# A hand-written order of all compute engines in the blocks of a gated state-space mixer

## The chip, the cores and the metric

The kernel runs on one core of one Trainium2 chip. The metric is the device time of one execution in microseconds, as a median over runs of the same kernel. TensorE (PE in the profile, its weight loads PEld) multiplies matrices into PSUM, VectorE (DVE) and ScalarE (ACT) work element by element, GpSimd (POOL) does too, and SyncE (SP) issues most DMAs. Each engine works through its own list of instructions in order and waits on semaphores for the others.

## What is computed

The reference is a transformer block on `x` of 4 x 256 rows of 512: attention, a sparse feed-forward, a state-space mixer and the feed-forward again, each added to `x`. The change lies in the mixer alone:

```
proj = norm(x) @ in_proj_w.T                 # gate (8192), x, B, C (8192 + 2*8*128), dt (128 heads)
xBC  = silu(conv1d(xBC, 4 taps) + conv_b)    # along time, per channel
hs, Bm, Cm = split(xBC)                      # 128 heads of 64, 8 groups of B and C, 128 wide
y    = ssd(hs, A, Bm, Cm, D, dt)             # y_i = sum_{j<=i} (C_i.B_j) exp(cum_i - cum_j) dt_j x_j + D x_i
g    = y * silu(gate)
g    = g * rsqrt(mean over each group of 1024 of g*g + eps) * norm_w
out  = g @ out_w.T                           # 8192 -> 512
```

In exact terms the reference goes through chunks of 32 steps. The kernel takes the quadratic form of the last but third line over all 256 steps of a sequence: positions `j` after `i` must add nothing (the mask).

## The kernel before, in words

The mixer's 8192 inner channels are 64 blocks of 128 (two heads each); 8 blocks are a group, which shares one B and one C. Products of two fp32 matrices are done as three fp32r matmuls of split operands (`split`: a rounded upper part by ScalarE, L105, and the rest by a subtraction on VectorE, L106; `mm3`, L113 to L115). So every weight, from `win` (tile `wr`) or `wout` (`wor`) and every recalled piece of `g` (`gr`) is split first, into `w`, `wo` and `gh`.

Block `i` goes through these steps:

- `projected`: x and then the gate of the block, 24 matmuls of 128x512 each, from the normed input `mx` into a PSUM tile `pp`.
- `conv`: ScalarE scales (L981), VectorE adds three taps (L988), ScalarE takes silu (L996) into `x2`. For B and C the same (`bc`, L993).
- `rows`, `differences`: for each head a row of cumulated sums is read from DRAM (`r`, L1031). VectorE subtracts columns (L1043, L1047), GpSimd adds the mask of -3e38 (`past`, L1044) on the four diagonal pieces, ScalarE takes exps (L1052 direct, L1056, L1057) into `em`. `weighted` (L1061) multiplies by the group's scores `gm`, which `scores` makes from B and C (L1013, copied by L1021).
- `turned`: 8 transposes of `x2` on TensorE (L1072), scaled by dt on VectorE (L1073) into `xd`.
- `product` (L1089): 64 small matmuls of `em` and `xd` into `pyy`; `gated` adds D x (L1101), multiplies by the gate's silu `gt` (L1211, L1104), spills `gb` to DRAM (L1106, issued by SP) and sums squares (ScalarE L1111 and L1113, GpSimd L1114).
- Out products of the group before: `recall` reads a spilled half (L1150), `partial` multiplies 24 matmuls into `pog`, `scaled` (L1162) adds them to `x`. There are 8 of them per group, one for each 128 rows. `root` (L1135 to L1141) makes the group's factor.

The loop `for i in range(NB + 1)` (L1198) writes block `i`'s x and gate with block `i-1`'s product. Of a group's eight blocks the first (`i % 8 == 0`) has no out product of the group before, the second has two (`PER`), the others one. B of the next group is projected behind block 6 of a group and C behind block 7, with their scores. This text doesn't fix the order: a planner places each engine's instructions by costs and due times, and only some are pinned. TensorE, VectorE, ScalarE, GpSimd and SP all get their lists this way in the mixer.

[...] two `pp` tiles of two banks each, one `pyy` of two banks, and a pool `ps` (tag "m") of two single banks that transposes, scores, sums and out products all share. `acc`, `gt` and `xd` have one buffer, `x2` two, `em` three, `r` four.

Of the kernel before, what the change touches and what calls it, by code (L numbers as in the profile page):

```python
# [9 lines left out]
F32 = mybir.dt.float32  # L10
F32R = mybir.dt.float32r
# [24 lines left out]


COLS = {}
_at = 0
for _name, _w in (  # L40
    ("ident", 128), ("neg", 128), ("rot", 128), ("bdk", 2), ("bdv", 128), ("idx", 1), ("past", 64),
):
    COLS[_name] = (_at, _at + _w)
    _at += _w
# [5 lines left out]
def constants():  # L50
# [8 lines left out]
    put("past", np.where(np.arange(Q)[None, :] < r[:, None] % Q, -3e38, 0.0).astype(np.float32))  # L59
# [18 lines left out]
def hybrid_kernel(  # L78
# [705 lines left out]
    def mixer(feed, later):  # L784
        with ExitStack() as es, ExitStack() as inner:
# [25 lines left out]
            def prepare(i):  # L811

                for n in range(i, i + 3):
                    fetch(n)
                if i < NW and i not in pieces:
                    pieces[i] = [pw.tile([P, KC, P], F32R, name=f"w{j}", tag=f"w{j}") for j in range(2)]
                    split(pieces[i], raws.pop(i), nc.gpsimd if i < 5 else nc.vector)
# [9 lines left out]
            past = w1.tile([P, Q], F32, name="past")  # L827
            load(past, cst[:, COLS["past"][0] : COLS["past"][1]])
# [9 lines left out]
            nc.gpsimd.memset(w1.tile([P, 360], F32, name="fill1"), 0.0)  # L838
# [64 lines left out]
            reset = p2.tile([P, NT], F32, name="reset", tag="sq")[:, :512]  # L903
# [69 lines left out]
            silus = []  # L973

            def conv(pp, ch, inner):
# [3 lines left out]
                    else po_.tile([P, NT], F32, name="bc", tag="gb", bufs=3)  # L979
# [12 lines left out]
                if not inner:  # L992
                    silus.append(nc.scalar.activation(acc, acc, AF.Silu).ins)  # L993
                    return acc
                x2 = p2.tile([P, NT], F32, name="x2", tag="x2", bufs=2)
                silus.append(nc.scalar.activation(  # L996
                    pair(x2).rearrange("p k u i -> p u k i"),
                    acc.rearrange("p (u k i) -> p u k i", u=2, i=Q), AF.Silu,
                ).ins)
                return x2  # L1000

            def scores(bt, ct):

                gm = p2.tile([P, 20, Q], F32, name="gm", tag="gm")
                for j in range(2):
                    for cs in ((0, 1), (2, 3)):
                        pg = ps.tile([P, 512], F32, name="pg", tag="m")
                        at = 0
                        for c in cs:
                            n = (4 - c) * Q  # L1010
                            for u in range(2):
# [4 lines left out]
                                )  # L1016
                            at += n
                        at = 0
                        for c in cs:
                            n = (4 - c) * Q  # L1020
                            nc.vector.tensor_copy(  # L1021
                                piece(gm, j, c), pg[:, at : at + n].rearrange("p (k i) -> p k i", i=Q)
                            )
                            at += n
                return gm

            def rows(h):

                r = p2.tile([P, 2 * L], F32, name="r", tag="r", bufs=4)
# [7 lines left out]
            def differences(h, r):  # L1037

                e = p2.tile([P, 20, Q], F32, name="em", tag="em", bufs=3)
                own, next_ = pieces_of(e, 0, 4, 4, 7), pieces_of(e, 1, 8, 2, 9)  # L1040
                rv = r.rearrange("p (j c i) -> p j c i", j=2, c=4)
                cv = col_t[:, h, :].rearrange("p (j c) -> p j c", j=2).unsqueeze(3)
                nc.vector.tensor_tensor(own, rv, cv.to_broadcast([P, 2, 4, Q]), ALU.subtract)  # L1043
                nc.gpsimd.tensor_tensor(  # L1044
                    own, own, past.unsqueeze(1).unsqueeze(1).to_broadcast([P, 2, 4, Q]), ALU.add
                )
                nc.vector.tensor_tensor(  # L1047
                    next_, rv[:, :, 1::2, :], cv[:, :, 0::2].to_broadcast([P, 2, 2, Q]), ALU.subtract
                )
                for j in range(2):  # L1050
                    for c in range(2):
# [3 lines left out]
                        )  # L1055
                nc.scalar.activation(next_, next_, AF.Exp)  # L1056
                nc.scalar.activation(own, own, AF.Exp)  # L1057
                return e
# [4 lines left out]
            def turned(n, x2):  # L1063

                xd = p2.tile([P, TT, P], F32, name="xd", tag="xd", bufs=1)
                for half in range(2):
                    yield xd
                    hs = slice(half * 4, half * 4 + 4)
                    tr = ps.tile([P, 4, P], F32, name="trx", tag="m")
                    for q in range(4):  # L1070
                        c = half * 4 + q
                        nc.tensor.transpose(tr[:, q, :], x2[:, c * P : (c + 1) * P], ident)  # L1072
# [6 lines left out]
                yield  # L1079
# [16 lines left out]
            def gated(n, x2, gt, py, sq):  # L1096

                gb = po_.tile([P, NT], F32, name="gb", tag="gb", bufs=3)
# [5 lines left out]
                nc.vector.tensor_tensor(gb, gb, gt, ALU.mult)  # L1104
                if n < NB - 1:
                    load(spill[(n // GB) % 2][n % GB], gb)  # L1106
                else:
                    last.append(gb)
                if sq is None:
                    sq = p2.tile([P, NT], F32, name="sq", tag="sq")  # L1110
                    nc.scalar.activation(sq, gb, AF.Square)  # L1111
                else:
                    nc.scalar.activation(x2, gb, AF.Square)  # L1113
                    (nc.gpsimd if n < NB - 1 else nc.vector).tensor_tensor(sq, sq, x2, ALU.add)  # L1114
                return sq
# [4 lines left out]
            def out_weights(g, k):  # L1120

                r = po_.tile([P, C], F32, name="wor", tag="wor", bufs=2)
                tc.keep_in_program_order(load(r, wout[g * GB + k]))
                n = g * GB + k
                w = [po_.tile([P, C], F32R, name=f"wo{j}", tag=f"wo{j}", bufs=GB) for j in range(2)]
                nc.scalar.activation(w[0], r, AF.Copy, scale=nw_s[:, n : n + 1])  # L1126
                nc.vector.scalar_tensor_tensor(
                    w[1], r, nw_s[:, n : n + 1], w[0].bitcast(F32), ALU.mult, ALU.subtract
                )
                return w  # L1130

            def root(sq):
                pq = ps.tile([P, TT], F32, name="pqs", tag="m")
                for t in range(TT):
                    nc.tensor.matmul(  # L1135
                        pq[:, t : t + 1], sq[:, t * P : (t + 1) * P], ones[:, 0:1], start=True, stop=True
                    )
                rg = rg_s.pop(0)
                rg_s.append(rg)
                nc.scalar.activation(rg, pq, AF.Sqrt, bias=eps, scale=1.0 / (GB * P))  # L1140
                nc.vector.reciprocal(rg, rg)  # L1141
# [233 lines left out]
```

## Time and profile before

| what | value |
| --- | --- |
| runs shown | 1930.27, 1933.32, 1936.76 us; median 1933.32 |
| the profiled execution | 1932.12 us, of which the span on the chip is 1930.3 |
| from 0 to 385 us (attention, feed-forward) | PE 343.1, DVE 251.8, ACT 238.1, POOL 112.5 busy, clock 0.96 |
| 385 to 1838 us (the mixer's blocks) | PE 1392.1, DVE 1172.6, ACT 1112.7, POOL 369.5 busy, clock 0.99 |
| 1838 to 1930 us (last out products, feed-forward) | PE 81.2, DVE 68.9, ACT 45.3, POOL 0 busy, clock 0.97 |
| GpSimd's mask, L1044, 128 of them | 229.9 us, mean 1800 ns (1272 to 3883) |
| table loads of ScalarE in the blocks | 265, each 1283 ns |
| VectorE's L1047, 128 of them | 409 ns at least, 419 median, 2611 at most |
| the three taps, L988 | 1241 to 1283 ns each |

The page's rows of groups give an engine, an operation, its operands by name, the count, the busy time with the mean of one, and behind a second bar how long the engine sat idle before it and what ended that. Rows in order of time give start, duration, engine, line, operation and operands; a bracket is the wait just before, with its releaser. A table load is the row in which ScalarE fetches the functions of another set: exp and silu lie in different sets here.

### The profile page before, as it was taken

Reading aid. Unit: us, or ns where it says so; the run is one execution under the profiler, and the core shown is the slowest. Engines: PE = TensorE matmul, PEld = TensorE weight load, DVE = VectorE, ACT = ScalarE, POOL = GpSimd, SP = SyncE. Lnnn points to the kernel's source line nnn. Section 1 sums busy time; section 2 is a strip of 40 time slices with the busy share of each in tenths; the row PEclk is TensorE's granted clock in tenths of the full one; section 3 lists DMA queues with packets and bytes.
Section 4 is the critical chain, followed back from the end, with each engine's and each line's share of the span. In section 5 each row is a group of like instructions: output and inputs, shape, how many; then the busy total and the mean of one; then the engine's idle time right before and its main releaser. Section 6 shows DMA issues by size and latency. Waiting matters only on the chain.

```text
span 1930.3 us, 33621 instructions
## 1 busy us (share of the span) xinstructions
PE 1816.3 (94%) x12882; PEld 1455.3 (75%) x12882; DVE 1493.3 (77%) x2157; ACT 1396.1 (72%) x2527; POOL 482.0 (25%) x380
## 2 busy tenths in 40 slices
PE   7999988889999999999999989999999999999997
PEld 6777767767677777787778778777887788778877
DVE  5666667688798879778878787877878878878877
ACT  6576675468898777787677777776787787677763
POOL 6332320013322222232222222222231232222200
PEclk9999999899999999999999999999999999999999
DMA  4000000033444434333434344443444434343241
GB/s 140 1 1 1 27 10 22 24 110 121 147 143 132 136 129 145 124 123 132 142 121 142 120 126 131 145 129 120 127 142 126 132 126 141 125 129 126 95 122 53
DMA packets 154834, 206.89 MB, mean 107 GB/s; under 512 B 14640, under 2 KB 79664, under 8 KB 154672
## 3 DMA queue, kind: packets, MB, share of 16 engines
q1 hardware_dynamic: 154672, 204.73, 33.7%
q8 instruction: 101, 1.65, 0.4%
q14 instruction: 61, 0.50, 0.1%
HBM read 169.03 MB, written 35.65 MB: 106 GB/s over the span
## 4 chain that ended last, share of the span: by engine, by line
PE 46%; DVE 21%; ACT 20%; issue 5%; DMA 4%; POOL 3%; SPq 0%; ACTq 0%; DVEq 0%; POOLq 0%
DVE acc L988 8%; PE pp L113 5%; PE pp L114 5%; PE pp L115 5%; PE pog L113 5%; PE pog L115 5%; PE pog L114 4%; ACT L996 2%; ACT x L996 2%; PE trx L1072 2%; PE pyy L1089 2%; ACT e L475 2%; DMA r<-cumd 2%; DVE em L1061 2%; POOL em L1044 2%
## 5 line engine op out<-in xcount | busy, mean ns | idle before, releaser
L1044 POOL TENSOR_TENSOR em<-em,past 128x512 f32<-128x512 f32 x128 | 229.9, 1800 | 1045.7 <-DVE em L1043 992.3
L113 PE MATMUL pp<-mx,w 128*128 128x512 f32 (+1 forms) x1160 | 467.0, 403 | 18.9 <-DVE acc L988 12.8
L115 PE MATMUL pp<-mx,w 128*128 128x512 f32 (+1 forms) x1160 | 454.3, 392 | 0.1
L114 PE MATMUL pp<-mx,w 128*128 128x512 f32 (+1 forms) x1160 | 453.9, 391 | 0.0
L1061 DVE TENSOR_TENSOR em<-em,gm 128x1280 f32<-128x1280 f32 x128 | 195.8, 1530 | 169.3 <-ACT em L1057 139.6
L113 PEld LDWEIGHTS pp<-mx,w 128*128 128x128 f32 x1160 | 218.8, 189 | 73.8 <-issue 13.4
L988 DVE SCALAR_TENSOR_TENSOR acc<-pp,cw_s,acc 128x1012 f32<-128x1012 f32 (+2 forms) x192 | 244.3, 1272 | 23.3 <-ACT acc L981 20.4
L115 PEld LDWEIGHTS pp<-mx,w 128*128 128x128 f32 x1160 | 218.9, 189 | 46.7 <-DVE w L106 0.5
L114 PEld LDWEIGHTS pp<-mx,w 128*128 128x128 f32 x1160 | 219.0, 189 | 40.6 <-issue 0.6
L113 PE MATMUL pog<-wo,gh 128*128 128x512 f32 x512 | 205.3, 401 | 2.5 <-ACT wo L1126 1.1
L1052 ACT ACTIVATE em<-r,end_t 128x128 f32<-128x128 f32 x512 | 169.2, 392 | 45.9 <-PE pyy L1089 45.2
L115 PE MATMUL pog<-wo,gh 128*128 128x512 f32 x512 | 200.1, 391 | 0.0
L114 PE MATMUL pog<-wo,gh 128*128 128x512 f32 x512 | 199.8, 390 | 0.0
L1089 PE MATMUL pyy<-em,xd 64*64 64x192 f32 (+3 forms) x4096 | 176.6, 310 | 13.9 <-DVE em L1061 13.9
L1089 PEld LDWEIGHTS pyy<-em,xd 64*64 64x64 f32 x4096 | 142.9, 138 | 58.5 <-issue 24.1
L996 ACT ACT_TABLE_LOAD x57 | 73.1, 1283 | 119.8 <-DVE acc L988 119.7
L105 ACT CAST w<-wr 128x512 fp32r<-128x512 f32 x144 | 88.3, 614 | 85.0 <-PE pp L114 81.1
L1114 POOL TENSOR_TENSOR sq<-sq,x 128x1024 f32<-128x1024 f32 x55 | 137.6, 2501 | 25.2 <-ACT x L1113 25.2
L475 ACT ACTIVATE e<-sc,nmx 128x256 f32<-128x256 f32 (+1 forms) x256 | 104.2, 442 | 21.0 <-DVE nmx L469 20.9
L113 PEld LDWEIGHTS pog<-wo,gh 128*128 128x128 f32 x512 | 96.1, 188 | 24.7 <-ACT rg L1140 2.0
L115 PEld LDWEIGHTS pog<-wo,gh 128*128 128x128 f32 x512 | 96.1, 188 | 20.8 <-DVE gh L106 0.3
L106 DVE TENSOR_TENSOR gh<-gr,gh 128x512 fp32r<-128x512 f32 (+1 forms) x128 | 86.0, 678 | 33.2 <-ACT gh L105 33.2
(294 smaller groups left out, 3463.3 us busy)
## 6 DMA issues: line engine op xcount, KB each, us to landing
wr<-in_win_dram SPq DMA_DIRECT2D x287, 256.0 KB, 2.9
r<-cumd SPq DMA_DIRECT2D x256, 128.0 KB, 3.0
spill<-gb SPq DMA_DIRECT2D x63, 512.0 KB, 2.6
gr<-spill SPq DMA_DIRECT2D x120, 256.0 KB, 3.2
wor<-in_wout_dram SPq DMA_DIRECT2D x64, 256.0 KB, 2.8
out_dram<-x SPq DMA_DIRECT2D x8, 256.0 KB, 2.4
x<-in_x_dram SPq DMA_DIRECT2D x1, 1536.0 KB, 8.9
gr<-spill SPq DMA_DIRECT2D x8, 192.0 KB, 2.8
```

What stands on the lines that cost most here:

```text
L105: nc.scalar.copy(hl[0], v)
L113: nc.tensor.matmul(o, lh, rh, start=(first and k == 0), stop=False)
L114: nc.tensor.matmul(o, lh, rl, start=False, stop=False)
L115: nc.tensor.matmul(o, ll, rh, start=False, stop=(last and k == n - 1))
L475: nc.scalar.activation(es_[c][:, 2 * j + pr, :], sc[:, j, :], AF.Exp, bias=nm[:, j : j + 1], accum_out=rs[:, c, h : h + 1],)
L988: nc.vector.scalar_tensor_tensor(av[:, :, d:], pv[:, :, : L - d], cw_s[:, ch, tap : tap + 1], av[:, :, d:], ALU.mult, ALU.add,)
L996: silus.append(nc.scalar.activation(pair(x2).rearrange("p k u i -> p u k i"), acc.rearrange("p (u k i) -> p u k i", u=2, i=Q), AF.Silu,).ins)
L1044: nc.gpsimd.tensor_tensor(own, own, past.unsqueeze(1).unsqueeze(1).to_broadcast([P, 2, 4, Q]), ALU.add)
L1052: nc.scalar.activation(piece(e, j, c, 2 - c, 2), rv[:, j, 2:, :], AF.Exp, bias=end_t[:, h, 2 * j + c : 2 * j + c + 1],)
L1061: nc.vector.tensor_tensor(e, e, gm, ALU.mult)
L1089: nc.tensor.matmul(py[d, u, j * L + c * Q : (j + 1) * L].rearrange("p (k i) -> p k i", i=Q), xd[us, 4 * j + c, d], piece(es2[hh], j, c)[us ...
L1114: (nc.gpsimd if n < NB - 1 else nc.vector).tensor_tensor(sq, sq, x2, ALU.add)
```

## The change

The planner no longer orders the blocks: a new function `block(i)` writes the instructions of one block for TensorE, ScalarE, VectorE and GpSimd in the order in which each engine is to take them (`manual_schedule`); SP's DMAs are still planned. Operations are cut so that they can be placed apart: `differences` and `exponentials`, the upper and lower part of each split, fetching and splitting, `silu` and `side_by_side`, `sums` and `root`, half projections.

- One out product stands in every block from block 9 on, with row tile `i % 8 - 1` (the last one of a group in the first block of the group after next). In the second block of a group it comes last.
- B of the next group is projected behind block 3 of a group and C behind block 4, both counted from 0; their convs stand in blocks 4 and 5, the scores in block 6.
- A block's exps are taken together at the start of the block after it, and its two silus together.
- The mask is no longer added: ScalarE clips the differences with relu (of the negative, then exp of the negative), and the scores `gm` are multiplied by a 0/1 triangle `tri` where they were copied.
- ScalarE issues the spill, two blocks later; `r` has two buffers for four; `gb` and `wor` have four; all weights of the start are split by GpSimd.

```diff
             def conv(pp, ch, inner):
...
-                if not inner:
-                    silus.append(nc.scalar.activation(acc, acc, AF.Silu).ins)
-                    return acc
+                return acc
...
-                            nc.vector.tensor_copy(
-                                piece(gm, j, c), pg[:, at : at + n].rearrange("p (k i) -> p k i", i=Q)
+                            nc.vector.tensor_tensor(
+                                piece(gm, j, c), apart(pg[:, at : at + n]), apart(tri[:, :n]), ALU.mult
                             )
...
-                nc.gpsimd.tensor_tensor(
-                    own, own, past.unsqueeze(1).unsqueeze(1).to_broadcast([P, 2, 4, Q]), ALU.add
-                )
...
+            def exponentials(h, e):
...
                 nc.scalar.activation(next_, next_, AF.Exp)
-                nc.scalar.activation(own, own, AF.Exp)
-                return e
+                nc.scalar.activation(own, own, AF.Relu, scale=-1.0)
+                nc.scalar.activation(own, own, AF.Exp, scale=-1.0)
+                if h + 2 < H:
+                    rr[h + 2] = rows(h + 2)
...
             def turned(n, x2):
...
+                trs = [ps.tile([P, 4, P], F32, name="trx", tag="m") for _ in range(2)]
+                for c in range(TT):
+                    nc.tensor.transpose(trs[c // 4][:, c % 4, :], x2[:, c * P : (c + 1) * P], ident)
...
+            def spilled(n, gb):
+                if n < NB - 1:
+                    nc.scalar.dma_start(spill[(n // GB) % 2][n % GB], gb)
...
+            def block(i):
+                g, gi = divmod(i, GB)
+                n = at["x", i]
...
+                out = (g - 1, gi - 1) if gi else (g - 2, TT - 1)
...
+                first_out = gi == 1
+                if i >= 2:
+                    spilled(i - 2, gbs[i - 2])
...
+                if late_:
+                    nc.vector.reciprocal(rgs[g - 1], rgs[g - 1])
+                    scaled(*late_.pop())
...
+                x_steps = projected("x", i)
+                next(x_steps)
+                next(x_steps)
+                if i:
+                    decays(i - 1)
+                waiting = [k for k in "bc" if k + "pp" in group]
+                for k in waiting:
+                    group[k] = conv(group.pop(k + "pp"), (NB if k == "b" else NB + G) + g + 1, False)
+                if i:
+                    turn(i - 1)
+                    weigh(i - 1)
+                acc = conv(next(x_steps), i, True)
+                if i >= 2:
+                    squared(i - 2, xs2.pop(i - 2), gbs.pop(i - 2))
+                done = outer(*out) if out and not first_out else None
+                lower.append(upper_piece(n + 2))
+                if g and gi >= 1:
+                    ss = {1: (1,), 2: (4, 5)}.get(gi, (2 * gi, 2 * gi + 1))
+                    lower.extend(upper_half(g - 1, s) for s in ss)
+                if g and gi == 1:
+                    lower.extend(upper_out((g - 1) * GB + k) for k in range(4, 8))
+                xs2[i] = side_by_side(acc)
+                for k in waiting:
+                    silu(group[k])
+                if done:
+                    scaled(*done)
+                lowered()
+
+                g_steps = projected("g", i)
+                next(g_steps)
+                if not done:
+                    next(g_steps)
+                if i:
+                    inner_products(i - 1)
+                if done:
+                    next(g_steps)
+                scoring = None
+                if gi == 6 and g + 1 < G:
+                    scoring = scores(group.pop("b"), group.pop("c"))
+                    gms[g + 1] = next(scoring)
+                    next(scoring)
+                    next(scoring)
+                pp = next(g_steps)
+                lower.append(upper_piece(n + 3))
+                if g and gi == 0:
+                    lower.append(upper_half(g - 1, 0))
+                    lower.extend(upper_out((g - 1) * GB + k) for k in range(4))
...
+                ems[i] = [differences(h) for h in (2 * i, 2 * i + 1)]
+                lowered()
...
+                nc.scalar.activation(gts[i], pp, AF.Silu)
+                if g and first_out:
+                    rgs[g - 1] = root(sums(g - 1))
+                    late_.append(outer(*out))
+                if gi in NEXT and g + 1 < G:
+                    group[NEXT[gi] + "pp"] = whole(projected(NEXT[gi], g + 1))
+                    upper_piece(n + 4)()
+
+            with tc.manual_schedule(
+                engines={e.engine for e in (nc.tensor, nc.scalar, nc.vector, nc.gpsimd)}
+            ):
+                for i in range(NB):
+                    block(i)
```

`decays(i)`, `turn(i)`, `weigh(i)` and `inner_products(i)` are block `i`'s exps, `turned`, `weighted` and `product` with `gated`. `projected` is now a generator that stops before, between and behind its two halves. `upper_piece`, `upper_half` and `upper_out` issue ScalarE's part of a split of `w`, `gh` and `wo` and return a function that issues VectorE's part and the fetch of a later one; `lowered()` calls those collected. `outer` is one out product, `NEXT` is `{3: "b", 4: "c"}`. Behind the loop stand the last block's exps, product and squares, the last out product of group 6 and the split of group 7's `wo`.

## The prediction

> **What bounds the kernel now.** I read the page's busy shares and slices first, then busy time by stretches, then TensorE's rows in order of time, and last the rows of ScalarE.
>
> ```profile
> PE 1816.3 (94%) x12882; PEld 1455.3 (75%) x12882; DVE 1493.3 (77%) x2157; ACT 1396.1 (72%) x2527; POOL 482.0 (25%) x380
> PE   7999988889999999999999989999999999999997
> PEclk9999999899999999999999999999999999999999
> ```
>
> TensorE (PE) leads, at nearly full clock. Its busy time counts overlapping matmuls, so what a full TensorE looks like must come from starts:
>
> ```profile
> 1016.69 0.39 PE L114 MATMUL pp<-mx,w 128*128 128x512 f32 x1
> 1016.92 0.39 PE L115 MATMUL pp<-mx,w 128*128 128x512 f32 x1
> 1017.23 2.41 PE L1089 MATMUL pyy<-em,xd 64*64 64x256 f32 x64
> 1019.58 0.50 PE L113 MATMUL pp<-mx,w 128*128 128x512 f32 x1
> ...
> 472.69:492.69 20.00, 18.42 (x134) 13.86 (x132) 14.82 (x20) 17.19 (x25) 7.03 (x5) 1.00 0.44 139
> 1371.33:1391.46 20.13, 20.05 (x145) 16.13 (x145) 16.33 (x20) 15.79 (x25) 5.80 (x3) 1.00 0.40 130
> ```
>
> A 128x512 matmul starts every 0.2275 us (20 of them in 4.55 us), though each row says 0.39. The 64 small ones of `product` cost 2.5 us with both changes of shape. The windows give busy PE, PEld, DVE, ACT, POOL: a block with an out product (1371 to 1391) is full of TensorE, while in group 0, without one (473 to 493), ScalarE is fullest and TensorE waits. The waits, in group 0 and then in one later group:
>
> ```profile
> 485.67 0.47 PE L113 MATMUL pp<-mx,w 128*128 128x512 f32 x1 [0.57 <-DVE acc L988]
> 488.01 1.09 PE L1072 MATMUL trx<-con,x 128*128 128x128 f32 x8 [0.28 <-ACT x L996]
> 494.06 0.50 PE L113 MATMUL pp<-mx,w 128*128 128x512 f32 x1 [0.73 <-ACT gt L1211]
> ...
> 1279.10 0.47 PE L113 MATMUL pp<-mx,w 128*128 128x512 f32 x1 [1.03 <-DVE acc L988]
> 1302.03 1.53 PE L1013 MATMUL pg<-bc 128*64 128x256 f32 x16 [2.67 <-ACT bc L993]
> 1322.92 4.07 PE L1089 MATMUL pyy<-em,xd 64*64 64x256 f32 x62 [2.52 <-DVE em L1061]
> ```
>
> Adding up TensorE's gaps over 0.25 us between 385 and 1930 gives 75 us: 26 before 590 (start and group 0), 46 in the later groups, 3 behind. All matmuls stay, so the change can win 75 us at most, and a few us of shorter gaps and of `product`s and scores cut in two, each with two more changes of shape. From block 9's `product` (606.05) to block 57's (1723.35) six groups take 1117.3 us, **186.2 each**.
>
> **TensorE's own work per group.** A block: 72 big matmuls x 0.2275 = 16.4, eight transposes 1.1 (470.71 to 471.66, with the return), `product` 2.5, so 20.0. Eight blocks are 160.0; B and C 48 x 0.2275 = 10.9; the scores 2.7; the sums of squares 1.8: 175.4. The new order balances the blocks (one out product in each, not none and two), but the mean work is the same; what counts is how much it waits.
>
> **A steady block of the changed order**, in us from its first x matmul, durations from the rows, with the 0.08 by which neighbours overlap:
> - PE: half x 2.7, transposes 3.8, half x 6.6, out product 12.0, `product` 14.6, g 20.0.
> - ACT: silu of the last gate 1.2; the spill's issue 1.5; table load 2.8; per head four exps 1.25, one of 256 0.31, relu 0.52 and exp 0.62, so two heads end at 8.3; x's scaling 9.5; later silu with its load.
> - DVE: xd 5.1, weighing head 0 7.0, head 1 8.3 + 1.5 = 9.8, three taps 13.7, `scaled` 14.4, three subtractions 16.2, gating 18.6, differences 20.5, one subtraction 21.1.
>
> `product` needs the weighing at 9.8 and is issued at 12.0: **2.2 us of slack**. VectorE ends 1.1 us into the next block and is needed there at 3.8. It has about 15.2 us of work in 20. So a steady block waits for nothing: 20.0 against 20.1 now.
>
> **Each edit.**
> - *GpSimd's add of the mask* (128 x 1.80 us) goes. The rows blame it for `em` waits (40.4 us), and VectorE's L1047 takes 2.61 at most against 0.41 at least while it runs; both go. Its cover was TensorE's out product in most blocks, so only the gaps shown above are worth time. ScalarE gets two relus, 1.04 us a block, inside the 8.3.
> - *Mask as a product in `scores`*: eight multiplies a group for eight copies (0.32 us mean); between equal cost and +0.1 each, behind TensorE; zero.
> - *Exps together, silus together*: 265 loads become 128, 137 x 1.28 = 175 us off ScalarE. In later groups TensorE covered them. [...] The rows:
>
> ```profile
> 1500.06 1.05 ACT L1113 ACTIVATE x<-gb 128x1024 f32<-128x1024 f32 x1
> 1501.12 1.28 ACT L1211 ACT_TABLE_LOAD   x1
> 1502.42 1.03 ACT L1211 ACTIVATE gt<-pp 128x1024 f32<-128x1024 f32 x1
> ```
>
>   The load starts 0.01 us after the square ends, and silu 0.02 after the load: 1.30, no drain. [...] I take the rows. [...] there it would shorten the chain by 1.0 us, which only the B and C blocks would feel. That relu needs no load beside exp no run here shows; [...] the new instruction list has no load there.
> - *Spill issued by ScalarE*: SP's row is 0.33 us; [...] I take 0.33, inside the slack. Behind it stand the exps.
> - *rows with two buffers*: a row is asked for when a head's exps end (8.3), lands 3.0 later, is needed at 18.6: covered by 7 us. SP's order is rows, wr, gr, gr, wr, each with its condition met in that order, so none blocks another.
> - *w, gh, wo prepared by hand*: same counts. wr is fetched a block ahead; the four wo of block 0 of a group end on VectorE 3.1 us into block 1, before xd at 3.8: free. In block 1 the out product comes last; `product` is asked for at 9.3 and em is there at 9.8: **0.5 lost**.
> - *B and C behind blocks 3 and 4* (counted from 0). This takes away the wait at 1302 (2.7). But in blocks 4 and 5 the B or C conv stands ahead of xd on VectorE, and its ScalarE scaling behind the exps. From the end of g: silu 1.2, a cast 1.7, spill 2.0, load 3.3, exps 8.7, scaling 9.9, taps 13.8, first xd 14.5. TensorE has done B or C (5.5), x and the transposes at 12.0, and the out product needs a bank that this xd frees (pool of two, both held by the transposes). **Wait 2.5 us, twice a group.** [...]
>
> **Sum.** A later group: 175.4 + 5.0 + 0.5 + 0.1 of semaphores for each of eight blocks = 181.7, against 186.2: six groups win 27 us. Group 0 is bound by ScalarE's circle: spill 0.3, load 1.3, exps 5.4, weighing 1.5, taps 3.9, load and silu 2.3, a cast 0.5, gate 1.0 = 16.3, against 17.3. But blocks 4 and 5 there take 25.2 (conv B 5.0, the weighing late by both xd and a whole second weighing 2.8, silu 1.0), block 8 19.5, and block 9 ends with an out product; added up, `product` of block 1 to that of block 9 is 161.7 against 159.7 (446.38 to 606.05): **2 lost**. The start stays with the dt chain of VectorE (to 413.1), which is unchanged: equal within 4. The end: last g to `product` 9 us later, as now (1831.7 to 1843.2 with its gaps): equal within 3. Altogether 1932.1 (the profiled execution, span 1930.3) - 27 + 2 = 1907; against the median of 1933.3 that is **1908 us**.
>
> **Rivals.**
> 1. *TensorE full* (0.12): if the B and C waits are hidden, 12 x 2.5 = 30 us more: 1878. For it: the windows show TensorE full where nothing is in front of it. Against: both queues are in written order, so nothing can pass the conv.
> 2. *ScalarE's chain too late* (0.15), slower: gate silu, load, exps with relu, weighing. Slack 2.2 us; each us beyond it costs 54 blocks 54 us and takes the win of 25 at 2.7. It would need relu and the exp behind it (same tile, so the second waits out the first) or the issue of the spill to cost 1.4 us a head more than their rows. At 3.2 the time is 1962. Against: every duration but the issue has a row.
> 3. *Win eaten by group 0 and the start* (0.18): the new list puts dt's transposes after 78 big matmuls, where TensorE has done 111 now before it waits for dcum; 33 x 0.2275 = 7.5 us may not be got back, and B and C waits of 3.5 add 12: 1928.
> 4. *Mask not gone from the path*: not possible, L1044 is not in the new list.
>
> The forecast itself (1895 to 1920) has 0.55. Faster by over 0.3% (below 1927.5; about what a measurement can tell from none) 0.77: the forecast, rival 1, and half of rival 3; within 0.3% 0.08; slower 0.15, rival 2. The range 1880 to 1940 leaves rival 2 out and the lower half of rival 1.
>
> **What would show it.** Right: no L1044 row; two loads a block; no gap before `pg`; starts of `product` 20.0 apart in steady blocks; a gap of 2 to 3 us before the out product of blocks 4 and 5, released by VectorE's xd. Wrong: gaps before `product` in every block (rival 2), no gap in blocks 4 and 5 (rival 1), more than 35 us of gaps before 610 (rival 3).

## The result and the profile after

The changed kernel takes 1908.86 us (median of 4 runs, 1907.48 to 1910.46); the kernel before, on the same chip, took 1932.3 (1930.27 to 1936.76). The ratio is 0.9876, with a 95% interval of 0.9856 to 0.9896. The profiled execution spans 1905.7 us against 1930.3. The forecast was 1908.

The experiments show that this number is the sum of two large parts of opposite sign, of which the forecast saw only the balance: the edits of the change are worth 76 us, and fixing the engines' order by hand, which came with them, costs 52.

A line of the kernel before has moved in the kernel after: `mm3` is L115 to L117, the taps of a convolution L1002, the weighing L1089, the transposes of x L1096, xd L1099, `product` L1115, the subtractions L1064 and L1065, the exps L1076 to L1084. These are the busy shares, TensorE's slices and the granted clock of the page after:

```profile
PE 1798.6 (94%) x12882; PEld 1463.3 (77%) x12882; DVE 1449.3 (76%) x2158; ACT 1280.1 (67%) x2520; POOL 246.7 (13%) x251
PE   7999988889899999999999999999999999999997
PEclk9999999899999999999999999999999999999999
```

TensorE's busy time hardly moves (1816.3 to 1798.6); GpSimd's halves and ScalarE loses 116 us, without any like change of the time. So the time does not follow either of them. What TensorE waits for stands in the page's costliest groups (busy us, mean ns, then idle time before it and its releaser):

```profile
L1148 POOL TENSOR_TENSOR sq<-sq,x 128x1024 f32<-128x1024 f32 x55 | 131.7, 2394 | 1284.1 <-ACT x L1147 1284.1
L115 PE MATMUL pog<-wo,gh 128*128 128x512 f32 x512 | 206.4, 403 | 28.8 <-DVE xd L1099 27.4
L1014 ACT ACT_TABLE_LOAD x63 | 80.8, 1283 | 164.5 <-DVE acc L1002 164.4
```

In the blocks GpSimd is left with the sums of squares alone. Of the 28.8 us before the out product `pog`, 27.1 are twelve waits, two in each of six groups, all released by xd. One of them, in TensorE's rows in order of time (start, duration, wait in brackets):

```profile
1189.98 0.39 PE L117 MATMUL pp<-mx,w 128*128 128x512 f32 x1
1192.59 0.51 PE L115 MATMUL pog<-wo,gh 128*128 128x512 f32 x1 [2.22 <-DVE xd L1099]
...
1193.41 0.58 PE L115 MATMUL pog<-wo,gh 128*128 128x512 f32 x1
1193.79 0.63 PE L116 MATMUL pog<-wo,gh 128*128 128x512 f32 x1
1194.21 0.63 PE L117 MATMUL pog<-wo,gh 128*128 128x512 f32 x1
1194.64 0.63 PE L115 MATMUL pog<-wo,gh 128*128 128x512 f32 x1
```

The matmul before it starts at 1189.98, so at a pace of 0.2275 us the next was due at 1190.21: it comes 2.38 us late. (Waits in the text are counted like this, from when the next matmul was due; the bracket counts from the end of a row and is 0.16 less.) Then TensorE runs on, but from 1193.4 to 1197 a matmul starts every 0.427 us instead of every 0.2275: nine slow ones cost 1.65 us more. Hence the block with B takes 29.37 us and that with C 27.75, from product to product, where both take 25.23 when nothing waits (below). VectorE and ScalarE in the same stretch:

```profile
1186.82 1.19 ACT L995 ACTIVATE bc<-pp,cb_s,cw_s 128x1024 f32<-128x1024 f32 x1
...
1188.04 3.90 DVE L1002 SCALAR_TENSOR_TENSOR bc<-pp,cw_s,bc 128x1012 f32<-128x1012 f32 x3 [7.16 <-ACT bc L995]
1191.86 1.28 DVE L1099 TENSOR_TENSOR xd<-trx,dt_t 128x512 f32<-128x512 f32 x2
1193.05 4.78 DVE L1089 TENSOR_TENSOR em<-em,gm 128x1280 f32<-128x1280 f32 x2
```

The transposes that xd reads started at 1186.60 and took 1.04. So xd could begin at 1187.64, 0.4 us before B's taps, but the text puts the three taps first, 3.9 us which nobody waits for soon. And VectorE had stood for 7.16 us until B's scaling, which ScalarE came to behind all the exps; the weighing of the first head, whose exps ended at 1184.25, had its place behind it too.

### The profile page after: what moved, and what is told of

Read it like the earlier page. It is cut to its first block, busy times and chain, and to the rows that moved or that the text cites. A ratio compares the mean times of both kernels' runs of the same rounds, so it can differ in the third digit from the quotient of the medians.

```text
span 1905.7 us, 33071 instructions
## 1 busy us (share of the span) xinstructions
PE 1798.6 (94%) x12882; PEld 1463.3 (77%) x12882; DVE 1449.3 (76%) x2158; ACT 1280.1 (67%) x2520; POOL 246.7 (13%) x251
## 2 busy tenths in 40 slices
DMA packets 134381, 169.71 MB, mean 89 GB/s; under 512 B 12240, under 2 KB 77392, under 8 KB 134224
## 3 DMA queue, kind: packets, MB, share of 16 engines
q8 instruction: 101, 1.65, 0.4%
## 4 chain that ended last, share of the span: by engine, by line
PE 68%; ACT 14%; DVE 13%; issue 3%; POOL 1%; DMA 1%; ACTq 0%; SPq 0%; DVEq 0%; POOLq 0%
PE pp L115 10%; PE pp L116 9%; PE pp L117 9%; PE pyy L1115 7%; PE pog L115 6%; PE pog L116 6%; PE pog L117 6%; DVE bc L1002 3%; ACT em L1076 3%; ACT e L477 2%; PE trx L1096 2%; DVE acc L1002 2%; ACT L1076 1%; DVE em L1089 1%; ACT em L1083 1%
## 5 line engine op out<-in xcount | busy, mean ns | idle before, releaser
L115 PE MATMUL pp<-mx,w 128*128 128x512 f32 (+1 forms) x1160 | 466.5, 402 | 7.7 <-DVE bc L1002 7.2
L117 PE MATMUL pp<-mx,w 128*128 128x512 f32 (+1 forms) x1160 | 454.0, 391 | 5.1 <-DVE w L830 5.1
L1148 POOL TENSOR_TENSOR sq<-sq,x 128x1024 f32<-128x1024 f32 x55 | 131.7, 2394 | 1284.1 <-ACT x L1147 1284.1
L1089 DVE TENSOR_TENSOR em<-em,gm 128x1280 f32<-128x1280 f32 x128 | 213.9, 1681 | 87.3 <-ACT em L1084 87.3
L115 PEld LDWEIGHTS pp<-mx,w 128*128 128x128 f32 x1160 | 219.5, 189 | 54.0 <-issue 4.2
L117 PEld LDWEIGHTS pp<-mx,w 128*128 128x128 f32 x1160 | 219.2, 189 | 51.2 <-DVE w L830 5.5
L1002 DVE SCALAR_TENSOR_TENSOR acc<-pp,cw_s,acc 128x1012 f32<-128x1012 f32 (+2 forms) x192 | 244.5, 1273 | 5.1 <-ACT acc L995 0.7
L115 PE MATMUL pog<-wo,gh 128*128 128x512 f32 x512 | 206.4, 403 | 28.8 <-DVE xd L1099 27.4
L116 PE MATMUL pog<-wo,gh 128*128 128x512 f32 x512 | 204.1, 399 | 0.0
L117 PE MATMUL pog<-wo,gh 128*128 128x512 f32 x512 | 203.8, 398 | 0.0
L1407 ACT ACTIVATE gt<-pp 128x1024 f32<-128x1024 f32 x64 | 65.8, 1028 | 175.1 <-PE pp L117 147.3
L1115 PEld LDWEIGHTS pyy<-em,xd 64*64 64x64 f32 x4096 | 136.6, 136 | 54.0 <-DVE em L1089 16.9
L1115 PE MATMUL pyy<-em,xd 64*64 64x256 f32 (+3 forms) x4096 | 166.0, 305 | 11.1 <-DVE em L1089 11.0
L1076 ACT ACTIVATE em<-r,end_t 128x128 f32<-128x128 f32 x512 | 163.3, 389 | 0.8
L1099 DVE TENSOR_TENSOR xd<-trx,dt_t 128x512 f32<-128x512 f32 x128 | 82.3, 685 | 81.8 <-PE trx L1096 81.8
L115 PEld LDWEIGHTS pog<-wo,gh 128*128 128x128 f32 x512 | 98.6, 193 | 54.6 <-DVE xd L1099 32.7
L1002 DVE SCALAR_TENSOR_TENSOR bc<-pp,cw_s,bc 128x1012 f32<-128x1012 f32 (+2 forms) x48 | 61.2, 1275 | 99.6 <-ACT bc L995 98.5
L117 PEld LDWEIGHTS pog<-wo,gh 128*128 128x128 f32 x512 | 98.6, 193 | 21.1
```

What stands on the lines that cost most here:

```text
L115: nc.tensor.matmul(o, lh, rh, start=(first and k == 0), stop=False)
L116: nc.tensor.matmul(o, lh, rl, start=False, stop=False)
L117: nc.tensor.matmul(o, ll, rh, start=False, stop=(last and k == n - 1))
L1002: nc.vector.scalar_tensor_tensor(av[:, :, d:], pv[:, :, : L - d], cw_s[:, ch, tap : tap + 1], av[:, :, d:], ALU.mult, ALU.add,)
L1076: nc.scalar.activation(piece(e, j, c, 2 - c, 2), rv[:, j, 2:, :], AF.Exp, bias=end_t[:, h, 2 * j + c : 2 * j + c + 1],)
L1089: nc.vector.tensor_tensor(e, e, gm, ALU.mult)
```

## The experiments

Two theories came first. **A:** the win comes from the order by hand, since TensorE is cut and stopped less often; what is left lies in the twelve waits. **Rivals:** it comes from the mask's leaving GpSimd, or from 135 table loads fewer, or from the edits (the spread of out products, where B and C stand, the later exps) whoever orders them. Each ratio below is to the kernel before on the same chip; differences in us are between medians, also across chips, on which the kernel before has medians of 1931.4 to 1935.6. So a difference of a few us is read from the ratios and their intervals.

**B's and C's taps behind xd.** The first moves `turn` alone, the second `turn` and `weigh`:

```diff
+                if i:
+                    turn(i - 1)
+                    weigh(i - 1)      # in the first run this stays below
                 for k in waiting:
                     group[k] = conv(group.pop(k + "pp"), ..., False)
-                if i:
-                    turn(i - 1)
-                    weigh(i - 1)
```

> In the blocks with a waiting B or C, VectorE makes xd ahead of that convolution's taps and weighs behind them. Theory (twelve out products wait 2.4 us each for the PSUM bank that xd frees): the twelve waits go, 28.6 us, 1880 us against 1908.9; xd ends about 10.6 us behind the last g, the taps at 14.5, the weighing at 17.5, just when the product is due at 17.4, so up to 0.5 us a time may come back (1880 to 1886). Rival (VectorE is what fills these blocks): the wait moves from the out product to the product, and the time stays above 1900.

Measured: 1892.6 us, 0.9789 (0.9765 to 0.9812), between the theory and the rival. The waits for the bank are gone, but the weighing now comes behind the taps, and `product` waits 1.25 and 1.55 us for it.

> As the run before, with the weighing too ahead of B's or C's convolution. Theory: the same 28.6 us go, now with some 4 us of slack for the product (weighing ends near 13.6, product due at 17.4): 1880 us. If the taps of the waiting convolution now reach the next x convolution, a wait of 1 us or more appears a block later: 1890 or more. Rival (VectorE fills these blocks): above 1900.

Measured: 1870.1 us, 0.9671 (0.9651 to 0.9692). A group now takes 174.4 us, and TensorE has no gap over 0.2 us in it. Busy time by stretches, one group each of the kernel after and of this one (length, then PE, PEld, DVE, ACT, POOL, the granted clock):

```profile
1154.00:1335.10 181.10, 176.66 (x1250) 144.12 (x1249) 143.76 (x178) 125.28 (x209) 16.77 (x7) 0.99 0.35 108
```

```profile
1132.00:1306.40 174.40, 174.40 (x1249) 143.04 (x1248) 139.80 (x178) 124.94 (x208) 16.82 (x7) 1.00 0.36 112
```

PE is busy for the whole 174.40. Six groups times 6.7 are 40 us where 28.6 were expected: a wait costs its gap and, in the B block, the slow matmuls behind it. The rest of the time hardly moves: from block 1's product to block 9's it is 162.7 us (162.2 in the kernel after).

**The same text, ordered by the planner.** The `manual_schedule` around the loop of blocks is taken away, nothing else:

```diff
-            with tc.manual_schedule(engines={...}):
-                for i in range(NB):
-                    block(i)
+            for i in range(NB):
+                block(i)
```

> The same instructions and buffers, but the engines' order in the blocks is left to the planner instead of the order of the text. Theory (the order by hand makes the win): 1925 us or more, with waits before product or pg again. Rival (the win is in the edits themselves: balance, where B and C stand, the mask, the loads): within 5 us of 1908.9.

Measured: **1856.7 us**, 0.9599 (0.9578 to 0.9621): 76 us faster than before (79 against the same chip's median), 52 faster than by hand, the fastest of all versions here. Theory A falls, and the rival had expected no gain either. A group takes 174.05 us, with a block of B or C at 25.2. So in the groups the planner has hardly more than the run before, and no slow matmul in them either. Its further lead lies in group 0 (154.1 us from block 1's product to block 9's, against 162.7) and around the last product (4.3 us), less 4.4 us by which block 1's product comes later. How the planner does it is in the rows around B in this kernel, ScalarE and then VectorE:

```profile
1153.84 0.61 ACT L1083 ACTIVATE em<-em 128x512 f32<-128x512 f32 x1
...
1160.83 1.19 ACT L995 ACTIVATE bc<-pp,cb_s,cw_s 128x1024 f32<-128x1024 f32 x1
...
1163.63 0.62 ACT L1083 ACTIVATE em<-em 128x512 f32<-128x512 f32 x1
...
1164.23 1.26 DVE L1002 SCALAR_TENSOR_TENSOR bc<-pp,cw_s,bc 128x1016 f32<-128x1016 f32 x1
1165.42 0.67 DVE L1099 TENSOR_TENSOR xd<-trx,dt_t 128x512 f32<-128x512 f32 x1
1166.02 1.26 DVE L1002 SCALAR_TENSOR_TENSOR bc<-pp,cw_s,bc 128x1020 f32<-128x1020 f32 x1
1167.20 0.67 DVE L1099 TENSOR_TENSOR xd<-trx,dt_t 128x512 f32<-128x512 f32 x1
```

B's scaling stands between the exps of the two heads (the two L1083) instead of behind both, and the halves of xd stand between B's taps. The price is on ScalarE, in the groups of its table loads (only the mixer's are shown):

```profile
L1076 ACT ACT_TABLE_LOAD x102 | 130.9, 1283 | 1.6
L1407 ACT ACT_TABLE_LOAD x62 | 79.5, 1283 | 1.1
L1014 ACT ACT_TABLE_LOAD x51 | 65.4, 1283 | 39.2 <-DVE acc L1002 39.0
L1084 ACT ACT_TABLE_LOAD x19 | 24.4, 1283 | 0.3
L1009 ACT ACT_TABLE_LOAD x15 | 19.2, 1283 | 0.3
```

With 5 more these are 254 loads against 130 by hand, and ScalarE is busy for 1452.4 us (78%). It is still faster, so fewer loads are not where the win lies.

**The mask back on GpSimd, in the order by hand.** Relu stays.

```diff
                 nc.vector.tensor_tensor(own, rv, cv.to_broadcast([P, 2, 4, Q]), ALU.subtract)
+                nc.gpsimd.tensor_tensor(
+                    own, own, past.unsqueeze(1).unsqueeze(1).to_broadcast([P, 2, 4, Q]), ALU.add
+                )
```

> The changed kernel, with GpSimd's add of the mask put back between the first subtraction and the exps (128 adds of about 1.8 us); everything else stays, relu included. Theory (GpSimd is off the path in this order): within 3 us of 1908.9. Rival [...]: 20 us or more slower, with second subtractions of up to 2.6 us again.

Measured: 1910.8 us, 0.9881 (0.9858 to 0.9904): no difference from the kernel after that the intervals could tell. VectorE pays, in the subtraction that the add runs beside: the group of the first subtractions after, and with the add back:

```profile
L1064 DVE TENSOR_TENSOR em<-r,col_t 128x512 f32<-128x512 f32 x128 | 87.5, 684 | 5.3 <-ACT col_t L965 5.3
```

```profile
L1067 DVE TENSOR_TENSOR em<-r,col_t 128x512 f32<-128x512 f32 x128 | 156.7, 1224 | 4.9 <-ACT col_t L968 4.9
```

That is 69 us of VectorE, most of it at a block's end, where VectorE has room. Not all: each later group has a new wait of 0.7 us before the transposes, released by VectorE's `scaled` (L1234), and in four groups C's wait is 0.4 longer, some 6 us together. Against that, only two of the twelve bank waits have slow matmuls behind them, not six, which gives back about as much (four times 1.65 us); where such stretches fell in the kernel after stands in the last section. The expectation named the second subtraction (L1071 here); it stays at 418 ns.

**Only the mask changed, in the kernel before.** The scores are also multiplied by `tri`, as in the kernel after.

```diff
-                nc.gpsimd.tensor_tensor(own, own, past..., ALU.add)
...
-                nc.scalar.activation(own, own, AF.Exp)
+                nc.scalar.activation(own, own, AF.Relu, scale=-1.0)
+                nc.scalar.activation(own, own, AF.Exp, scale=-1.0)
```

> The kernel before, with only the mask changed: no add on GpSimd, relu on ScalarE, the scores multiplied by 0 and 1; the planner's order stays. Theory (the mask is off the path there too, but for stretches of VectorE): 1926 to 1934 against 1932.3. Rival (the mask's removal is the win): 1912 or less.

Measured: 1926.2 us, 0.9970 (0.9961 to 0.9980): 6.6 us. The waits for `em` shrink, but a steady block grows from 20.11 to 20.6, with 0.7 us before the transposes for x's silu: the two relus are on that path.

**Two table loads more, in the order by hand.**

```diff
                 for h, e in zip((2 * i, 2 * i + 1), ems[i]):
+                    if h % 2:
+                        nc.scalar.activation(fill1[:, 0:1], fill1[:, 1:2], AF.Silu)
                     exponentials(h, e)
```

> The changed kernel, with one silu of a single column between the exps of the two heads, which adds two table loads to ScalarE's chain ahead of the weighing. Theory (a load costs 1.3 us and no drain; 2.2 us of slack in a steady block): the chain is 2.7 longer, so 0.5 in each of some 36 steady blocks, 2.7 in each of the twelve with B or C and in six of group 0: 18 + 32 + 16 = 66 us, 1975. [...] Rival (loads are not on the path at all): 1909.

Measured: 2045.3 us, 1.0586 (1.0569 to 1.0603), 70 above the theory's sum. ScalarE's rows between two heads of this kernel:

```profile
1264.79 0.63 ACT L1085 ACTIVATE em<-em 128x512 f32<-128x512 f32 x1
1265.44 1.28 ACT L1305 ACT_TABLE_LOAD   x1
1266.74 0.20 ACT L1305 ACTIVATE fill<-fill 128x1 f32<-128x1 f32 x1
1266.94 1.28 ACT L1077 ACT_TABLE_LOAD   x1
1268.24 1.28 ACT L1077 ACTIVATE em<-r,end_t 128x128 f32<-128x128 f32 x4
```

The load starts 0.02 us after the exp ends, and nothing stands between them. From the last exp of one head to the first of the next it is 3.45 us, where the kernel after has 0.53: the chain is 2.9 us longer. Of the five steady blocks in a group two lose nothing and three 0.6. In the kernel after, the second weighing ends 2.0 to 3.9 us ahead of its product in these blocks: that is their slack, of which 2.2 had been counted. The sum fell short elsewhere: the bank waits grow from 2.38 to 6.07 and 5.31, with 14 and 7 slow matmuls behind them, and the second block of a group gets a wait of 4.31 for the weighing. A group takes 198.0 instead of 181.1.

**Silu's table loaded early.**

```diff
                 acc = conv(next(x_steps), i, True)
+                nc.scalar.activation(fill1[:, 0:1], fill1[:, 1:2], AF.Silu)
```

> The changed kernel, with a silu of a single column right behind x's scaling, so that silu's table is loaded while VectorE works the taps. Theory (in group 0 ScalarE's circle sets the period of 16.4 us, the load of 1.28 among it; elsewhere loads are covered): 1.2 us in each of seven blocks, 8 us, 1901. Rival (VectorE closes the circle in group 0): 1908.

Measured: 1916.9 us, 0.9925 (0.9910 to 0.9941), 8 us slower: a miss on both sides. The block of group 0 that took 16.39 us still takes 16.39, so the load ahead of silu is not in the circle that sets it. The first eight intervals between `product`s sum to 153.1 us instead of 149.3, one later group to 1.6 more, and the stretch from the last `product` on is 3 longer. Much of it is the clock: behind the first product the profile has 57.0 us at a granted clock of 0.50, the kernel after 45.2, which makes up to 5.9 us. The later group's 1.6 is one such stretch more, from 1590.38 to 1593.80 behind its wait for C. Why the waits of group 0 shift, no run tells.

**Relu on VectorE.**

```diff
-                nc.scalar.activation(own, own, AF.Relu, scale=-1.0)
-                nc.scalar.activation(own, own, AF.Exp, scale=-1.0)
+                nc.scalar.activation(own, own, AF.Exp)
 ...
+                nc.vector.tensor_scalar(own, own, 0.0, None, ALU.min)   # end of differences
```

> The changed kernel, with relu replaced by a minimum with 0 on VectorE behind the subtractions, and the plain exp behind it. Theory: the chain of exps is 1.04 us shorter: 1.0 in each of the twelve waits of B and C and in some six blocks of group 0, nothing in steady blocks, and VectorE's two minima (about 0.4 us each) at the block's end are covered: 18 us, 1891. Rival (VectorE pays what ScalarE saves): 1905 to 1915.

Measured: 1874.2 us, 0.9701 (0.9685 to 0.9716): 35 us, twice the 18 expected. A group takes 177.1, six of them 24 us less. The bank waits are 1.05 and 1.74 instead of 2.38, and now no slow matmuls follow: together 3.6 a group; the second block's product comes 0.4 earlier. In group 0 the block of 16.38 us falls to 14.35, so the exps are in the circle that sets it; from block 1's product to block 9's it is 155.6 us instead of 162.2.

**Parts taken back, in the planner's order.** With the order as winner out of the way, which edit makes the 76 us? First where B and C stand, then the spread of the out products, then the mask (the add of the diff above). The planner plans anew for each text, so a run shows an edit together with the order that the planner finds for it:

```diff
-NEXT = {3: "b", 4: "c"}
+NEXT = {6: "b", 7: "c"}
...
-                if gi == 6 and g + 1 < G:
+                if gi == 0 and g:
                     scoring = scores(group.pop("b"), group.pop("c"))
```

> The changed kernel in the planner's order (1856.7), with B and C again behind blocks 6 and 7 of a group and the scores in the first block of the next. Theory (before, the scores stood right behind C's convolution, and TensorE waited 2.7 us for them and 2.5 more for the weighing in each group; placing B and C earlier is most of the 12 us a group): 5 to 8 us a group come back, seven times: 1892 to 1913. Rival (where B and C stand is worth nothing once the planner orders the text): 1854 to 1862.

Measured: 1863.7, 0.9641 (0.9623 to 0.9659): 7.0 us, so the theory of 5 to 8 us a group falls. A group takes 175.3 us, with two waits of 0.4 us around the transposes of one block.

```diff
-                if out[0] < 0:
+                if out[0] < 0 or gi == 0:
                     out = None
...
+                if gi == 7 and g:
+                    scaled(*outer(g - 1, TT - 1))
```

> The changed kernel in the planner's order (1856.7), with two out products in the last block of a group and none in the first, as before the change. Theory (a block without an out product has 14.4 us of TensorE's work, less than ScalarE's and VectorE's, so TensorE waits there): 1.5 to 3 us a group, 1866 to 1877. Rival (the planner moves the out product's matmuls to where TensorE would wait): 1854 to 1860. Rival (the even spread is most of the win): 1890 or more.

Measured: 1863.7, 0.9649 (0.9630 to 0.9669): 7.0 us, between the rival and the theory. A group takes 174.8 us.

> The changed kernel in the planner's order (1856.7), with GpSimd's add of the mask put back (relu stays). Taking that add away won 6.6 us in the kernel before, and putting it back cost nothing in the order by hand. Theory (TensorE is full here, and the mask is beside the path): 1855 to 1861. Rival (the planner's order has the exps soon behind the subtractions, so the 1.8 us stand in ScalarE's chain): 1864 or more.

Measured: 1878.4, 0.9727 (0.9711 to 0.9743): 21.7 us, so the mask does matter when the planner orders the text; the rival is right that it is on the path. The groups of the weighing in the planner's order, without and with GpSimd's add:

```profile
L1089 DVE TENSOR_TENSOR em<-em,gm 128x1280 f32<-128x1280 f32 x128 | 190.2, 1486 | 73.0 <-ACT em L1084 68.6 <-ACT em L1081 2.3
```

```profile
L1095 DVE TENSOR_TENSOR em<-em,gm 128x1280 f32<-128x1280 f32 x128 | 221.3, 1729 | 84.4 <-ACT em L1090 82.3
```

A weighing takes 0.24 us more beside GpSimd's adds and starts later; a group grows to 175.8, with waits of about 1 us for xd in a block with B, and the rest, some 8 us, is lost in the first two groups.

> The changed kernel in the planner's order (1856.7) with all three parts back at once: the mask's add on GpSimd, B and C behind blocks 6 and 7, two out products in one block and none in the next. One by one they cost 21.7, 7.0 and 7.0 us. Theory (they add up, and what is left of the 76 us lies in the rest of the text: exps and weighing one block later, the buffers, each input weight fetched once): 1892, 1885 to 1900. Rival (each covers for the others, and together they are the whole win): 1920 or more.

Measured: 1869.2, 0.9671 (0.9649 to 0.9694): 12.5 us, less than the mask alone. They do not add up, and all three undone still leave 63 of the 76 us. One group of this kernel is 174.7 us without a gap over 0.25. So the largest share lies in what the text keeps in all these versions: exps, transposes and weighing are written at the start of the block that needs them, not at the end of the one before; splits, fetches and spill stand elsewhere; buffers are divided otherwise; and each input weight is fetched once. What the traces show of it is lead. In a steady block (28) of this kernel the second weighing starts 11.9 us ahead of its product, against 4.7 in the kernel before, and x's silu 8.6 us ahead of the transposes, against 1.1. That fits the waits that are gone (in a later group before: some 2.7 us for the scores' silu, 1.7 to 2.5 for the weighing, 1.0 for taps that hold a bank, 0.5 for x's silu). Which of the kept parts gives the lead was not tried.

## Why the prediction was right

- **TensorE bounds, and its waits are what can be won.** Right: the versions without waits in a group take 174.1 to 174.4, and 175.4 had been counted. That the best version wins 76 us, where a bound of 75 had been set, is luck. The six later groups give 73 of them (186.2 to 174.05 each), though their gaps had been counted as 46; group 0 and the start together give 1.4 of the 26 counted there. What the gaps leave out, in the six groups before: nine stretches of 3.41 us at a granted clock of 0.50 (up to 15 us), and 0.3 us in a steady block (20.11 against 19.79).
- **A steady block of 20.0 with 2.2 us of slack.** 19.79 by the trace, with 2.0 to 3.9 of slack. The order of the steps was right.
- **B and C: 2.5 us twice a group, for the bank that xd frees.** The gap is 2.38 eleven times and 2.80 once, with that releaser. The term left out the slow matmuls behind one wait in each group (a start every 0.427 us instead of 0.2275, 1.65 us a group).
- **0.5 us in the second block of a group.** 0.4 (17.47 us against 17.07 with relu on VectorE).
- **A later group 181.7; six win 27.** 181.1; they win 30.5. TensorE's own work had been set 1.0 too high, and the slow matmuls 1.65 too low; that these two nearly cancel is luck.
- **Group 0 loses 2.** From block 1's `product` to block 9's it is 162.2 us for 161.7 predicted, against 159.7. The single blocks scatter more: those without B or C that were set at 16.3 take 15.2 to 18.2. (Its chain of 16.3 adds up to 16.2, and in its window of group 0 TensorE is the fullest, with 18.42 us of 20.00, not ScalarE with 17.19; that ScalarE's chain sets these blocks is borne out by relu's move.)
- **The end equal within 3: wrong.** From block 57's `product` to the last instruction it is 211.7 against 206.95, a loss of 4.8. 2.6 of it are lost at the last `product`, of which two matmuls go ahead and 62 wait (it ends 21.9 us behind the one before it, not 19.3), and 3.7 behind it (88.7 us to the end, not 85.0); five steady blocks give 1.6 back. In the kernel before, the kernel after, and the planner's order:

```profile
1838.23 0.64 PE L1089 MATMUL pyy<-em,xd 64*64 64x256 f32 x2
1841.57 0.73 PE L113 MATMUL pog<-wo,gh 128*128 128x512 f32 x2 [1.12 <-ACT wo L1126]
1843.16 2.40 PE L1089 MATMUL pyy<-em,xd 64*64 64x256 f32 x62
```

```profile
1808.11 0.64 PE L1115 MATMUL pyy<-em,xd 64*64 64x256 f32 x2
1810.07 0.49 PE L115 MATMUL pog<-wo,gh 128*128 128x512 f32 x1 [1.32 <-ACT wo L1165]
1812.78 4.54 PE L1115 MATMUL pyy<-em,xd 64*64 64x256 f32 x62 [2.22 <-DVE em L1089]
```

```profile
1763.84 2.41 PE L1115 MATMUL pyy<-em,xd 64*64 64x256 f32 x64
```

  After, TensorE waits 2.22 us for the weighing, and then the 62 matmuls take 4.54 us instead of 2.40: from 1811.27 to 1818.10 the granted clock is 0.50. The planner's order is ahead of the one by hand at this product alone; behind it, it takes 90.2 us. Why the end is longer in both, no run tells.
- **The mask costs nothing on the path.** True of the order by hand in sum (1.9 us, within the intervals), where some 6 us of new waits met fewer slow matmuls. It is worth 6.6 in the kernel before and 21.7 in the planner's order, so it was no property of the edit.
- **Table loads: no gain, and nothing in front of a load.** Right: 0.02 us in the rows above, and the fastest version has 254 of them. Relu needed no load of its own here: none stands at its line (L1083); the exp behind it on the same tile starts 0.03 us after it ends (1183.59 and 1183.62). The loads by hand are 130, not 128.
- **Relu would be better on VectorE by 1.0 a block, in the B and C blocks alone.** Direction right; 35 us instead of 12, because group 0's circle runs through the exps as well, and no slow matmuls follow the shorter waits (1.05 and 1.74 us).

In sum 30.5 - 1.1 (block 9's `product` comes later) - 4.8 = 24.6 us, the difference of the spans. In the blocks the path, the waits and their size were the ones forecast; that the total came within 1 us owes something to errors that cancel. (The chances named for "faster" add up to 0.76, not 0.77.) What the working did not ask was what the text could do in another order. It followed the order as written, compared it with the order before, and so put down to the change as a whole what the edits had won and the order had partly given away. Rival 1, TensorE full at 1878, was given little chance; the kernel gets past it with two lines of the fixed order moved (1870), and further without that order (1857).

## What to carry to other kernels

When a change fixes an order and edits the work at once, run the edits under the old ordering too: here they are worth 76 us and the order costs 52. In an order written by hand, look for short work that others wait for behind long work that they don't: xd stood behind 3.9 us of taps, and moving two lines won 39 us. Price an operation in the order it will stand in: the same add on GpSimd cost 2, 7 or 22 us.

## What was not expected of the hardware

- **Behind waits of the same length TensorE's pace halved or not, and where the wait fell went with it.** In the traces of the kernel before and the kernel after, the stretches at half clock (0.50 granted) in the blocks are 3.413 us long, or twice that, and within each trace they begin whole multiples of 3.413 us apart. The kernel after, cut along this grid around the wait for xd in a B block (up to 1192.59) and that in the C block of the same group (up to 1221.96); the granted clock is the number behind POOL:

```profile
1190.05:1193.46 3.41, 1.19 (x6) 0.72 (x5) 3.37 (x5) 3.05 (x4) 0.76 (x1) 1.00 0.00 0
1193.46:1196.87 3.41, 3.41 (x10) 2.64 (x9) 3.41 (x2) 0.12 (x1) 1.63 (x1) 0.50 0.00 0
...
1217.35:1220.77 3.42, 2.39 (x11) 1.65 (x9) 3.28 (x3) 1.02 (x2) 0.00 (x0) 1.00 0.04 11
1220.77:1224.18 3.41, 2.21 (x10) 1.84 (x11) 3.41 (x4) 2.19 (x4) 2.10 (x1) 1.00 0.00 0
1224.18:1227.60 3.42, 3.42 (x16) 2.60 (x14) 3.42 (x3) 0.62 (x1) 0.30 (x1) 1.00 0.00 0
```

  Both waits are 2.38 us. B's lies in one stretch, of which TensorE is busy 1.19 us, and the next stretch has half the clock. C's lies across a border, with 2.39 and 2.21 us busy, and nothing follows. So it is with all twelve: in five groups out of six B's wait lies in one stretch, and 9 or 10 slow matmuls follow, while C's is cut; in the first of the six B's is cut, and C's (2.80) lies in one stretch but for 0.1 us. In these two traces, from block 1's product to the last, each of the 15 full-clock stretches with 2.09 us or more of TensorE's idle time is followed by one at half clock, as are 2 of the 13 with 1.40 to 1.86 us, and none with less. Counted from the start of the span, the grid lies at 2.21 us (modulo 3.413) in the kernel after and at 2.48 in the kernel before. So a few us of difference between versions with such waits can be luck: an estimate, from 1.65 us behind each wait that lies in one stretch, once a group in six groups.
- **With GpSimd's add back, VectorE's rows take up to 1.8 times as long**: 684 to 1224 ns for the 128x512 subtraction in the order by hand, 1486 to 1729 for the mean weighing in the planner's; beside one add of squares (GpSimd, from 1192.70, 2.39 us), two weighings took 4.78 us, where the run with them ahead of the taps has 2.88.
- **The kernel before fetched input weights twice**: 287 fetches of 256 KB against 145, 206.89 MB moved against 169.71. What that cost, no run tells.
